# A two-layer graph network: retrieval from the memory computed one stage later, beside the sums of the same state

## The chip, the cores and the metric

The kernel runs on one core of a Trainium2 chip. The core has TensorE (matmuls, results in PSUM), VectorE, ScalarE, GpSimd and SyncE; in the profile they are PE (weight loads: PEld), DVE, ACT, POOL and SP. Each works through its own queue of instructions in order. Transfers run on 16 DMA engines and are issued from the queues of SP, ACT (plain copies) and POOL (gathers with a list of indices). The time is that of one execution on the device, in microseconds (us).

## The reference

32768 nodes with 128 features, 524288 edges (`src`, `dst`). Layer 0 is a graph layer with attention, layer 1 is three steps of a memory layer; the change touches layer 1 alone:

```python
for _ in range(T):                                   # T = 3, ALPHA = 0.5, coeff = 0.2
    q = x @ Wq.T + bq
    attn = softmax(BETA * (q @ keys.T), axis=-1)     # 512 keys
    retrieved = attn @ values
    lap = _laplacian_term(x, row, col)               # x - dinv * sum over edges of dinv * x
    x = (1.0 - ALPHA) * x + ALPHA * (retrieved - coeff * lap)
mu = jnp.mean(x, axis=-1, keepdims=True); var = jnp.var(x, axis=-1, keepdims=True)
return (x - mu) * rsqrt(var + EPS) * ln_w + ln_b
```

After it x is the layer norm of (x1 + this), x1 being layer 1's input. Of a state x, a step thus needs two things that don't depend on each other: the retrieval (with 0.4 x, called `part` in the kernel) and the sum over the edges. The next state is `part` plus that sum.

## The kernel before

A block is 512 nodes (64 blocks), a window 128 nodes (256 windows, four in a block). Every fp32 row is split into three bf16 rows, so that the sums over edges run as bf16 matmuls.

The edges are handled in two halves. **Spread**: for each window of source rows, six groups of matmuls with a 0/1 matrix `pick` (line 1448) copy the rows into slots, two PSUM banks a group; each group is cast to `y_o` (line 1453) by ScalarE or, for every `share`-th group, by VectorE, and half a window is stored to DRAM (line 1456, SP). **Sums**: for each window of target rows, 19 matmuls accumulate in PSUM (`add`, line 1486, matmul at 1495): five with rows gathered by GpSimd (`listed`, line 1470), two with shared gathered rows (`common`), twelve with slots loaded from DRAM (`y_i`, line 1461). The 0/1 matrix `oh` for them is a comparison on VectorE (line 1481). When a window's sums are done, VectorE adds them to `part` (`close`, line 2174, three operations at 2179).

`Sums.steps` (line 1520) gives the order within a window: ask for the slots and gathers `lead` windows ahead, first add, `oh` for a later window, then the other adds, with one extra function after every fourth add where the caller hands some in, and `close` at the end.

Layer 1 has four stages:

1. *First spreads* (pool `l1p`, line 2209). Layer 0's output is normalized (`first`), stored to `xs_d[0]`, multiplied with `dinv` and split (`prepare`, line 2068), and spread (`emit`, line 2094; `share` 2, two PSUM buffers `exp`). The retrieval for the same state runs beside it.
2. and 3. *Middle stages* (pool `l1w`, line 2234), t = 0 and 1: sums of state t (`consume`, line 2165), and, two blocks behind, preparation, spreads and retrieval of the new state t + 1. `weave` (line 1041) mixes the two lists of steps.
4. *Last stage* (pool `l1z`, line 2259): sums of state 2 and the two layer norms at the end (`finish`, line 2187), whose four pieces for the block before go as the extra functions, one in each window: moments; normalize, scale, shift and add x1; moments; normalize and store.

The retrieval of a block is `project` (transposes), `query` (matmul with Wq), four times `scores` (matmul with the keys, maximum on VectorE at line 1061, Exp on ScalarE at 1063) and `turn` (transposes, copy to `pt`), `retrieve` (matmul with the values) and `remain` (transposes, division, 0.4 x, store of `part` to `part_d`). Their places within the 24 steps of a block's spreads are numbers beside them (line 2147). In the stages with sums, `ask_part` (line 2154) loads `part` a block ahead on ScalarE's queue.

In stages 1 to 3 a scheduler orders each engine's instructions around this; in the last stage the order is the written one:

```python
with tc.manual_schedule():                       # line 2264
    ask_part(t, 0, wp)
    sums = Sums(exs[t], wp, p_g, ramp, 6, 2)     # lead 6, oh two windows ahead
    ends = []
    for b in range(NB):
        st = {}
        run(consume(t, b, st, sums, wp, ends))
        ends = finish(b, st, wp)
    run(ends)
```

Of the kernel before, what the change touches and what calls it, by code (L numbers as in the profile page):

```python
# [28 lines left out]
AHEAD = 2  # L29
UNROLL = 4  # L30
# [879 lines left out]
def tile_gnn_resnorm(ctx: ExitStack, tc: tile.TileContext, a: dict, out: bass.AP):  # L910
# [1100 lines left out]
    def layer1_grid(v_d, s3, c3):  # L2011

        exs = [Exchange("src", slots_d[t % 2], rows_d[t]) for t in range(T_STEPS)]
        with tc.tile_pool(name="l1g", bufs=1) as gp:
# [53 lines left out]
            def prepare(t, b, st, wp, p_s, p_tr):  # L2068

                ex = exs[t]  # L2070

                def rows():
                    nx = wp.tile([P, NCH, D], F32, name="nx")
                    nc.vector.tensor_tensor(nx, st["x"], dinv[:, b * NCH:(b + 1) * NCH].unsqueeze(2)
                                            .to_broadcast([P, NCH, D]), OP.mult)
                    st["r"], st["split"] = ex.split_steps(wp, b, nx, nx)

                def project():
                    ps = p_tr.tile([P, NCH, P], F32, name="tr")
                    for c in range(NCH):  # L2080
                        nc.tensor.transpose(ps[:, c, :], st["x"][:, c, :], ident)
                    st["xT"] = wp.tile([P, BLK], F32, name="xT")
                    nc.scalar.copy(st["xT"], ps.rearrange("p c n -> p (c n)"))

                def query():
                    ps = p_s.tile([P, BLK], F32, name="s")
                    nc.tensor.matmul(ps, w["WqT"], st["xT"], start=True, stop=True)
                    st["q"] = wp.tile([P, BLK], F32, name="qT")
                    nc.scalar.activation(st["q"], ps, AF.Identity, bias=v["L1_gnn_bq"])
                return [(1, rows), (2, project), (4, lambda: st["split"][0]()), (7, query),  # L2090
                        (8, lambda: st["split"][1]()), (10, lambda: st["split"][2]()),
                        (14, lambda: st["split"][3]())]

            def emit(t, b, st, wp, p_e, p_s, p_tr, share):

                ex = exs[t]
                y = {}

                def scores(c):
                    if c == 0:  # L2100
                        st["pt"] = wp.tile([P, NCH, BLK], F32, name="pt")
                        st["sums"] = wp.tile([P, NCH], F32, name="sums")
                    s = p_s.tile([P, BLK], F32, name="s")
                    nc.tensor.matmul(s, st["q"][:, c * P:(c + 1) * P], keysT, start=True, stop=True)  # L2104
                    st["pr", c] = softmax_rows(wp, s, st["sums"][:, c:c + 1])
# [19 lines left out]
                def remain():  # L2125
                    ps = p_tr.tile([P, NCH, P], F32, name="tr")
                    for c in range(NCH):
                        nc.tensor.transpose(ps[:, c, :], st["oT"][:, c * P:(c + 1) * P], ident)
                    part = wp.tile([P, NCH, D], F32, name="part_o")
                    nc.vector.tensor_tensor(part, ps, st["rec"].unsqueeze(2).to_broadcast([P, NCH, D]), OP.mult)  # L2130
                    nc.vector.scalar_tensor_tensor(part, st["x"], 0.4, part, op0=OP.mult, op1=OP.add)
                    nc.sync.dma_start(kept_of(part_d, b), flat(part))

                def spread(n):
                    c, m = divmod(n, KS)
                    i = b * NCH + c
                    if m == 0:
                        ask_pick(wp, i + 2)
                    ex.spread(wp, p_e, "exp", i, picked[i], st["r"][:, c, :], m, y, n % share == share - 1)
                    if m == KS - 1:  # L2140
                        del picked[i]

                places = [(n, lambda n=n: spread(n)) for n in range(NCH * KS)]
                return places + [(0, lambda: scores(0)), (3, lambda: scores(1)), (5, lambda: turn(0)),
                                 (6, lambda: scores(2)), (8, lambda: turn(1)), (9, lambda: scores(3)),
                                 (11, lambda: turn(2)), (13, lambda: turn(3)), (17, retrieve), (20, remain)]

# [4 lines left out]
            parts = {}  # L2152

            def ask_part(t, b, wp):

                if b < NB:
                    p_i = wp.tile([P, NCH, D], F32, name="part_i", bufs=3)
                    nc.scalar.dma_start(flat(p_i), kept_of(part_d, b))
                    parts[b] = [p_i]
                    if t == T_STEPS - 1:  # L2160
                        x1 = wp.tile([P, NCH, D], F32, name="x1", bufs=3)
                        nc.scalar.dma_start(flat(x1), kept_of(xs_d[0], b))
                        parts[b].append(x1)

            def consume(t, b, st, sums, wp, extra=()):

                extra = list(extra) + [None] * NCH

                def begin():
                    ask_part(t, b + 1, wp)  # L2170
                    st["part"], *st["x1"] = parts.pop(b)
                    st["x"] = wp.tile([P, NCH, D], F32, name="xn", bufs=5)

                def close(ps, c):
                    i = b * NCH + c
                    acc = st["part"][:, c, :]
                    for o in range(3):
                        dst = st["x"][:, c, :] if o == 2 else acc
                        nc.vector.scalar_tensor_tensor(dst, ps[:, o * D:(o + 1) * D], dinv01[:, i:i + 1],  # L2179
                                                       acc, op0=OP.mult, op1=OP.add)  # L2180

                steps = [begin]
                for c in range(NCH):
                    steps += sums.steps(b * NCH + c, lambda ps, c=c: close(ps, c), [extra[c]] if extra[c] else [])
                return steps

            def finish(b, st, wp):
# [8 lines left out]
                def sum_up():  # L2196
                    st["a"][1]()
                    nc.vector.tensor_add(st["x2"], st["x2"], st["x1"][0])
# [10 lines left out]
            with tc.tile_pool(name="l1p", bufs=2) as wp, \  # L2209
                    tc.tile_pool(name="l1p_exp", bufs=2, space=PSUM) as p_e, \  # L2210
                    tc.tile_pool(name="l1p_s", bufs=2, space=PSUM) as p_s, \
# [4 lines left out]
                for n in range(-NCH - 3, NB):  # L2216
# [10 lines left out]
                    if 0 <= n + 1 < NB:  # L2227
                        lists.append(prepare(0, n + 1, sts[n + 1], wp, p_s, p_tr))
                    if n >= 0:
                        lists.append(emit(0, n, sts[n], wp, p_e, p_s, p_tr, 2))  # L2230
# [3 lines left out]
            with tc.tile_pool(name="l1w", bufs=2) as wp, \  # L2234
# [4 lines left out]
                for t in range(T_STEPS - 1):  # L2239
                    sums = Sums(exs[t], wp, p_g, gc["iota1"], 2)  # L2240
                    sts = {}
                    ask_part(t, 0, wp)
                    for w0 in range(2):
                        ask_pick(wp, w0)
                    for n in range(-2, NB):
                        lists = []
                        if n + 1 in sts:
                            lists.append(prepare(t + 1, n + 1, sts[n + 1], wp, p_s, p_tr))
                        if n >= 0:
                            lists.append(emit(t + 1, n, sts[n], wp, p_e, p_s, p_tr, 4))  # L2250
                        two_b = placed(*lists)
                        b = n + 2
                        if b < NB:
                            sts[b] = {}
                            weave(two_b, consume(t, b, sts[b], sums, wp))
# [3 lines left out]
            with tc.tile_pool(name="l1z", bufs=2) as wp, \  # L2259
                    tc.tile_pool(name="l1z_r", bufs=1, space=PSUM) as p_r, \  # L2260
                    tc.tile_pool(name="l1z_seg", bufs=4, space=PSUM) as p_g:
                t = T_STEPS - 1
                ramp = ramp_in_psum(p_r)
                with tc.manual_schedule():
                    ask_part(t, 0, wp)
                    sums = Sums(exs[t], wp, p_g, ramp, 6, 2)
                    ends = []
                    for b in range(NB):
                        st = {}
                        run(consume(t, b, st, sums, wp, ends))  # L2270
# [91 lines left out]
```

## Time and profile before

| what | value |
| --- | --- |
| median of 3 runs | 13194.35 us (13187.15 to 13196.0) |
| profiled execution, its time | 13193.95 us |
| its span, first to last instruction | 13192.2 us |
| busy in the span: PE, DVE, ACT, POOL | 11231.3, 9517.9, 6589.1, 6302.2 us |
| first spreads, about 5725 to 7180 us | 1455 us |
| middle stages, to 9345 and to 11504 us | 2165 and 2159 us |
| last stage, to the end | 1688 us |

The stages' bounds are read from the first and last instructions of their lines. The shares of busy time over the whole span are averages over stages with different limits, so that each stage is read for itself. A group in the profile is named by its line, its engine, its operation and the tiles it writes and reads (out<-in); "idle before" is the time that the engine stood still just before these instructions, with what it waited for. In the timeline the first number is the start, the second the duration.

### The profile page before, as it was taken

Reading aid. Unit: us, or ns where it says so; the run is one execution under the profiler, and the core shown is the slowest. Engines: PE = TensorE matmul, PEld = TensorE weight load, DVE = VectorE, ACT = ScalarE, POOL = GpSimd, SP = SyncE. Lnnn points to the kernel's source line nnn. Section 1 sums busy time; section 2 is a strip of 40 time slices with the busy share of each in tenths; the row PEclk is TensorE's granted clock in tenths of the full one; section 3 lists DMA queues with packets and bytes.
Section 4 is the critical chain, followed back from the end, with each engine's and each line's share of the span. In section 5 each row is a group of like instructions: output and inputs, shape, how many; then the busy total and the mean of one; then the engine's idle time right before and its main releaser. Section 6 shows DMA issues by size and latency. Waiting matters only on the chain. (4 is left out here: it accounts for less than half of the span.)

```text
span 13192.2 us, 164703 instructions
## 1 busy us (share of the span) xinstructions
PE 11231.3 (85%) x57831; PEld 5536.4 (42%) x57831; DVE 9517.9 (72%) x15195; ACT 6589.1 (50%) x10238; POOL 6302.2 (48%) x5525
## 2 busy tenths in 40 slices
PE   7798798666679988889997999999899999866666
PEld 2233233232334444344443555555455555433333
DVE  7977977899777777678886666666566666566666
ACT  4455455677712222368885666666566666500000
POOL 0084075000077777300001666666566666477777
PEclk9999899999889999999999999999999999988888
DMA  1000000688899999778887999999999999988887
GB/s 43 10 15 19 10 14 16 252 321 323 324 307 316 322 319 320 254 259 309 305 311 293 396 400 400 399 397 397 352 400 398 396 401 399 363 299 290 289 290 255
DMA packets 1410558, 3689.71 MB, mean 280 GB/s; under 512 B 219827, under 2 KB 634707, under 8 KB 1408563
## 3 DMA queue, kind: packets, MB, share of 16 engines
q1 hardware_dynamic: 969712, 2969.23, 59.8%
q0 software_dynamic: 252608, 520.41, 12.5%
q10 hardware_dynamic: 187394, 189.42, 4.4%
q8 instruction: 457, 7.49, 0.2%
q14 instruction: 387, 3.16, 0.1%
HBM read 2175.76 MB, written 1502.58 MB: 279 GB/s over the span
## 5 line engine op out<-in xcount | busy, mean ns | idle before, releaser
L1470 POOL DMA_INDIRECT listed<-rows,other x5120 | 5291.4, 1033 | 4127.8 <-issue 3138.3
L1453 ACT CAST y_o<-exp 128x768 bf16<-128x768 f32 x4224 | 3234.0, 805 | 1162.2 <-PE exp L1448 784.7
L1495 PEld LDWEIGHTS <-oh 128*128 128x128 bf16 x19456 | 1970.8, 102 | 2570.0 <-issue 1529.6
L1448 PE MATMUL exp<-rows,pick 128*128 128x384 bf16 x10752 | 2426.5, 328 | 380.3 <-ACT y_o L1453 223.2
L1495 PE MATMUL seg<-y_i,oh 128*128 128x384 bf16 x12288 | 2563.4, 345 | 20.4 <-DMA y_i<-slots 19.7
L1453 DVE CAST y_o<-exp 128x768 bf16<-128x768 f32 x1920 | 1831.8, 954 | 690.5 <-PE exp L1448 559.1
L1495 PE MATMUL seg<-listed,oh 128*128 128x384 bf16 (+1 forms) x5120 | 1313.3, 335 | 801.7 <-DMA listed<-rows,other 780.5
L1448 PEld LDWEIGHTS <-pick 128*128 128x128 fp8e4 x10752 | 1045.7, 98 | 1729.8 <-issue 1162.7
L1661 ACT ACTIVATE pT<-s 128x1024 f32<-128x1024 f32 x1024 | 1048.4, 1025 | 1378.5 <-PE s L1636 957.5
L1641 DVE TENSOR_REDUCE mx<-s 128x2 f32<-128x1024 f32 x1024 | 1246.3, 1221 | 358.4 <-PE s L1636 357.9
L2179 DVE SCALAR_TENSOR_TENSOR part_i<-seg,dinv,part_i 128x128 f32<-128x128 f32 x1536 | 532.4, 347 | 1337.9 <-PE seg L1495 1319.2
L1657 PE MATMUL s<-ql,k 32*128 32x512 f32 x4096 | 1217.9, 673 | 167.8 <-DVE mx L1641 154.6
L1636 PE MATMUL s<-k,q 32*128 32x512 f32 x4096 | 1222.5, 676 | 9.3 <-DVE mx L1641 4.9
L1481 DVE TENSOR_TENSOR oh<-iota,slot 128x2432 bf16<-128x2432 bf16 x768 | 1087.3, 1416 | 3.0 <-DMA slots<-y_o 3.0
L1084 ACT ACTIVATE ln_rs<-ln_mv,eps_c 128x4 f32<-128x4 f32 x128 | 38.0, 297 | 1637.7 <-DVE ln_mv L1082 1637.7
L2104 PE MATMUL s<-keysT,qT 128*128 128x512 f32 x1536 | 793.7, 598 | 2.0 <-ACT pr L1063 1.4
L2116 PE MATMUL s<-pt,values 128*128 128x512 f32 x1536 | 720.4, 594 | 2.1 <-ACT pt L2111 2.0
L1495 PE MATMUL seg<-common,oh 128*128 128x384 bf16 (+1 forms) x2048 | 607.9, 350 | 50.9 <-DMA common<-rows,shared 50.8
L1657 PEld LDWEIGHTS s<-ql,k 32*128 32x128 f32 x4096 | 320.7, 191 | 763.2 <-DVE mx L1641 314.5
L1392 POOL MEMSET rows<- 128x8 bf16 x64 | 6.7, 106 | 1260.4 <-PE exp L1448 749.7
L1061 DVE TENSOR_REDUCE nm<-s 128x1 f32<-128x512 f32 x768 | 523.6, 684 | 105.6 <-PE s L2104 103.7
L1063 ACT ACTIVATE pr<-s,nm 128x512 f32<-128x512 f32 x768 | 536.3, 698 | 114.9 <-DVE nm L1061 112.1
(410 smaller groups left out, 14178.5 us busy)
## 6 DMA issues: line engine op xcount, KB each, us to landing
slots<-y_o SPq DMA_DIRECT2D x2048, 576.0 KB
y_i<-slots SPq DMA_DIRECT2D x1024, 1152.0 KB
pick<-pick SPq DMA_DIRECT2D x1024, 192.0 KB
listed<-rows,other POOLq DMA_INDIRECT x5120
rows<-rows SPq DMA_DIRECT2D x192, 384.0 KB
band<-row_dst SPq DMA_DIRECT2D x128, 384.0 KB
band<-row_src ACTq DMA_DIRECT2D x256, 192.0 KB
part_d<-part_o SPq DMA_DIRECT2D x192, 256.0 KB
```

Source lines behind the costliest of these rows:

```text
L1063: nc.scalar.activation(pr, s, AF.Exp, bias=nm, accum_out=sums)
L1448: nc.tensor.matmul(ps[:, j, :ROW], pick[:, o:o + P], r, start=True, stop=True)
L1453: (nc.vector.tensor_copy if to_dve else nc.scalar.copy)(dst, ps[:, :, :ROW])
L1470: nc.gpsimd.indirect_dma_start(out=g[:, k, :], out_offset=None, in_=self.table, in_offset=bass.IndirectOffsetOnAxis(ap=index[:, k:k + 1], ...
L1481: nc.vector.tensor_tensor(oh.rearrange("p c (w z) -> p c w z", z=2), ramp.rearrange("p (w z) -> p w z", z=2)[:, None].to_broadcast([P, NC2 ...
L1495: nc.tensor.matmul(ps[:, :n], oh[:, j, :], src, start=(k == 0), stop=(k == NC2 - 1))
L1636: nc.tensor.matmul(ps[:, s % 2, :], t["q", o][32 * s:32 * s + 32, c * P:(c + 1) * P], t["k", o][32 * s:32 * s + 32, :], start=True, stop=True)
L1641: nc.vector.tensor_reduce(m[:, c, 2 * i:2 * i + 2, xr[o]], st[b].pop(("two", i)), AX.X, OP.max, negate=True)
L1657: nc.tensor.matmul(ps[:, s % 2, :], t["k", o][32 * s:32 * s + 32, c * P:(c + 1) * P], t["ql", o][32 * s:32 * s + 32, :], start=True, stop= ...
L1661: nc.scalar.activation(t["p", c][:, 2 * i:2 * i + 2, :], ps, AF.Exp)
L2104: nc.tensor.matmul(s, st["q"][:, c * P:(c + 1) * P], keysT, start=True, stop=True)
L2116: nc.tensor.matmul(ps, values[:, k, :], st["pt"][:, k, :], start=(k == 0), stop=(k == NCH - 1))
```

## The change

The retrieval for state t leaves the stage that makes state t and goes to the stage that sums it: out of the first spreads, from state t + 1 to state t in the middle stages, and new into the last stage. Its functions are the same; they are taken out of `prepare` and `emit` into `memory`, which gives a front (`project`, `query`) and a back (the rest).

- Each middle and last stage loads the states themselves (`ask_state`, `x_i`, three blocks ahead, on ScalarE's queue), from `xs_d[0]`, `part_d` and `xs_d[1]`, and the middle stages store the state that they finish (`close`, on SP's queue) where `remain` stored `part`. `part` stays on the chip.
- Before the first block of a stage `first_states` computes the whole retrieval of block 0 and the front of block 1. From then on, beside the sums of block b, stand the back of block b + 1 and the front of block b + 2 (`ahead`).
- In the first spreads the PSUM banks of the retrieval go to a third `exp` buffer, and every third cast is VectorE's (before: every second).
- In the last stage there are 16 places in a block, one after every fourth add; the pieces of the layer norms stand first in places 0, 4, 8 and 12, the steps of the retrieval at two thirds of their old numbers. The PSUM buffers of the sums go from 4 to 3, two each go to the retrieval's `s` and `tr`, and slots and gathers are asked for 5 windows ahead and not 6.

```diff
-            def prepare(t, b, st, wp, p_s, p_tr):
+            def prepare(t, b, st, wp):
...
+            def memory(st, wp, p_s, p_tr, bufs):
                 def project():
                     ps = p_tr.tile([P, NCH, P], F32, name="tr")
                     for c in range(NCH):
-                        nc.tensor.transpose(ps[:, c, :], st["x"][:, c, :], ident)
+                        nc.tensor.transpose(ps[:, c, :], st["xi"][:, c, :], ident)
...
-                    part = wp.tile([P, NCH, D], F32, name="part_o")
+                    st["part"] = part = wp.tile([P, NCH, D], F32, name="part")
                     nc.vector.tensor_tensor(part, ps, st["rec"].unsqueeze(2).to_broadcast([P, NCH, D]), OP.mult)
-                    nc.vector.scalar_tensor_tensor(part, st["x"], 0.4, part, op0=OP.mult, op1=OP.add)
-                    nc.sync.dma_start(kept_of(part_d, b), flat(part))
+                    nc.vector.scalar_tensor_tensor(part, st["xi"], 0.4, part, op0=OP.mult, op1=OP.add)
+
+                return ([(2, project), (7, query)],
+                        [(0, lambda: scores(0)), (3, lambda: scores(1)), (5, lambda: turn(0)),
+                         (6, lambda: scores(2)), (8, lambda: turn(1)), (9, lambda: scores(3)),
+                         (11, lambda: turn(2)), (13, lambda: turn(3)), (17, retrieve), (20, remain)])
...
+            states = [xs_d[0], part_d, xs_d[1]]
+            def ask_state(t, b, wp, p_s, p_tr):
                 if b < NB:
+                    st = {"xi": wp.tile([P, NCH, D], F32, name="x_i", bufs=3)}
+                    nc.scalar.dma_start(flat(st["xi"]), kept_of(states[t], b))
+                    st["front"], st["back"] = memory(st, wp, p_s, p_tr, 1 if t == T_STEPS - 1 else 2)
+                    mems[b] = st
+            def first_states(t, wp, p_s, p_tr):
+                for b in range(3):
+                    ask_state(t, b, wp, p_s, p_tr)
+                run(f for _, f in mems[0]["front"] + mems[0]["back"] + mems[1]["front"])
+            def ahead(b):
+                lists = [mems[b + 1]["back"]] if b + 1 < NB else []
+                return lists + ([mems[b + 2]["front"]] if b + 2 < NB else [])
...
+                    if c == NCH - 1 and t < T_STEPS - 1:
+                        nc.sync.dma_start(kept_of(states[t + 1], b), flat(st["x"]))
...
-                    tc.tile_pool(name="l1p_exp", bufs=2, space=PSUM) as p_e, \
-                    tc.tile_pool(name="l1p_s", bufs=2, space=PSUM) as p_s, \
+                    tc.tile_pool(name="l1p_exp", bufs=3, space=PSUM) as p_e, \
...
-                        lists.append(emit(0, n, sts[n], wp, p_e, p_s, p_tr, 2))
+                        lists.append(emit(0, n, sts[n], wp, p_e, 3))
...
-                        two_b = placed(*lists)
                         b = n + 2
+                        two_b = placed(*lists, *ahead(b))
...
-                    tc.tile_pool(name="l1z_seg", bufs=4, space=PSUM) as p_g:
+                    tc.tile_pool(name="l1z_s", bufs=2, space=PSUM) as p_s, \
+                    tc.tile_pool(name="l1z_tr", bufs=2, space=PSUM) as p_tr, \
+                    tc.tile_pool(name="l1z_seg", bufs=3, space=PSUM) as p_g:
...
-                    sums = Sums(exs[t], wp, p_g, ramp, 6, 2)
+                    sums = Sums(exs[t], wp, p_g, ramp, LAST, 2)
+                    first_states(t, wp, p_s, p_tr)
...
+                        slots = [[] for _ in range(4 * NCH)]
+                        for c, f in enumerate(ends):
+                            slots[4 * c].append(f)
+                        for at, f in sorted((x for one in ahead(b) for x in one), key=lambda x: x[0]):
+                            slots[at * 4 * NCH // (NCH * KS)].append(f)
+                        extra = [[lambda fs=fs: run(fs) for fs in slots[4 * c:4 * c + 4]] for c in range(NCH)]
+                        run(consume(t, b, st, sums, wp, p_s, p_tr, extra))
```

`LAST` is 5.

## The prediction

> **What bounds the kernel now.** I first cut the span into the stages of layer 1 with the view of busy time by stretch. The rows are the spreads of layer 0 (for comparison), the first spreads of layer 1, the two middle stages and the last stage.
>
> ```profile
> core 0: us, PE busy (x) PEld busy (x) DVE busy (x) ACT busy (x) POOL busy (x), PEclk, DMA share, GB/s
> 2383.00:3622.00 1239.00, 830.86 (x3720) 375.37 (x3720) 1082.30 (x1478) 928.20 (x1317) 12.27 (x68) 0.93 0.88 321
> 5725.00:7180.00 1455.00, 1296.33 (x6016) 688.42 (x6016) 1256.51 (x2320) 1152.98 (x1967) 0.00 (x0) 0.99 0.84 306
> 7180.00:9345.00 2165.00, 2067.13 (x10605) 1155.32 (x10606) 1303.93 (x2109) 1346.24 (x2230) 1400.54 (x1333) 0.99 1.01 390
> 9345.00:11504.00 2159.00, 2070.16 (x10646) 1156.81 (x10644) 1307.59 (x2115) 1359.84 (x2251) 1360.49 (x1291) 1.00 1.01 391
> 11504.00:13192.00 1688.00, 1088.27 (x4864) 540.95 (x4864) 1077.29 (x2880) 39.32 (x129) 1264.36 (x1312) 0.81 0.85 286
> ```
>
> Three different limits show. The first spreads (1455 us) have TensorE at 89%, VectorE at 86%, ScalarE at 79% and transfers at 84%: no single one is full, the engines hand work to each other. The middle stages have full transfers (share 1.01). The last stage has nothing full by these columns, ScalarE almost idle, and a granted clock of 0.81. Next I read the waits of the last stage (waiter, waited for, us in total, times, longest).
>
> ```profile
> DVE part_i L2179 <- PE seg L1495: 547.6, 151, 17.5
> PE seg L1495 <- DMA listed<-rows,other: 532.5, 350, 5.5
> POOL listed L1470 <- issue: 336.6, 1105, 0.3
> ```
>
> TensorE waits for gathered rows, and GpSimd, which issues the gathers, waits for nobody: 0.3 us between one gather and the next. So GpSimd bounds this stage: 1312 gathers at 0.95 + 0.3 = 1.25 us are 1640 us. By the timeline a window of the sums takes 6.50 us here (1456.5 us for 224 windows), a block of four 26.0 us. A window is 19 accumulating matmuls ("adds").
>
> Then the groups of the first spreads (count | busy us, mean ns | idle before), for the prices of what moves:
>
> ```profile
> L1453 DVE CAST y_o<-exp 128x768 bf16<-128x768 f32 x768 | 733.1, 955 | 136.3 <-PE exp L1448 119.9 <-ACT pt L2111 4.0 <-ACT y_o L1453 2.8
> L1453 ACT CAST y_o<-exp 128x768 bf16<-128x768 f32 x768 | 615.3, 801 | 229.4 <-PE exp L1448 195.4 <-ACT xT L2083 9.0 <-DMA slots<-y_o 7.6
> L1063 ACT ACTIVATE pr<-s,nm 128x512 f32<-128x512 f32 x256 | 178.0, 695 | 15.0 <-DVE nm L1061 12.4
> L1061 DVE TENSOR_REDUCE nm<-s 128x1 f32<-128x512 f32 x256 | 174.1, 687 | 40.9 <-PE s L2104 40.0
> L1063 ACT ACT_TABLE_LOAD x16 | 20.5, 1283 | 0.3
> ```
>
> And last the timeline of VectorE over one window of the last stage (start, us, operation), since the change puts work into this queue:
>
> ```profile
> 12330.22 0.74 DVE L2179 SCALAR_TENSOR_TENSOR part_i<-seg,dinv,part_i 128x128 f32<-128x128 f32 x2 [4.73 <-PE seg L1495]
> 12331.00 0.35 DVE L2179 SCALAR_TENSOR_TENSOR xn<-seg,dinv,part_i 128x128 f32<-128x128 f32 x1
> 12331.26 1.42 DVE L1481 TENSOR_TENSOR oh<-ramp_p,slot 128x2432 bf16<-128x2432 bf16 x1
> 12332.59 0.17 DVE L1088 RECIPROCAL ln_rs<-ln_rs 128x4 f32<-128x4 f32 x1
> 12332.80 1.11 DVE L1090 TENSOR_SCALAR x<-xn,ln_mv,ln_rs 128x128 f32<-128x128 f32 x4
> 12333.95 0.69 DVE L1093 TENSOR_TENSOR x<-x,ln_w 128x512 f32<-128x512 f32 x1
> 12334.67 0.69 DVE L1094 TENSOR_TENSOR x<-x,ln_b 128x512 f32<-128x512 f32 x1
> 12335.40 0.69 DVE L2198 TENSOR_TENSOR x<-x,x 128x512 f32<-128x512 f32 x1
> 12336.01 0.73 DVE L2179 SCALAR_TENSOR_TENSOR part_i<-seg,dinv,part_i 128x128 f32<-128x128 f32 x2
> ```
>
> The reader is to see an order that can't be swapped: the close of a window waits for its last add, then come the comparison `oh` (1.33 us to the next start) and a piece of the layer norms (here 3.42 us), and only then anything that stands behind them.
>
> **The change, part by part.** The profiled execution took 13193.95 us (span 13192.2, 1.75 us around it), 0.4 us below the median of the runs; the sum goes from 13194.
>
> *First spreads.* Away go, per block, 4 reductions of 0.69 us and 1.7 us of remainder on VectorE, 4 Exp of 0.70 + 0.20 and 7 copies or Identity of 0.6 to 0.7 on ScalarE, the matmuls between them, and one 256 KB store on SP's queue. Casts go from 768 : 768 to 1024 on ScalarE and 512 on VectorE. New sums: ScalarE 1024 x 0.801 = 820 plus 52 (vT), 80 (rows) and 5 (square root) = 957; VectorE 512 x 0.955 = 489 plus about 353 (norm, moments, rows) = 842; TensorE under 700. Transfers: 0.84 x 1455 = 1222 us of engine time for 446 MB; without the 64 stores (16.8 MB) 1176. So the transfers become the floor. How near does the stage come? The middle stages reach a share of 1.01, which gives 1164; the layer 0 spreads, also with three PSUM buffers, 0.88, which gives 1336; with no better coupling than now it is 1400. Layer 0's VectorE was 87% busy, here it would be near 67%, so I take a share of 0.93, 1265 us: **-190** (ends -291 and -55).
>
> *Middle stages.* The same retrieval runs, on the state that is summed and not the one that is spread; 64 loads of `x_i` for 64 of `part_i` on ScalarE's queue, 64 stores of the state for 64 of `part_d` on SP's, both waiting for the same kind of VectorE result. Transfers stay full, so the middle costs nothing either way; if the transfers had room, TensorE at 95% would still hold it. The edges change: after the last sums the last two blocks are spread, 53 us from 11449.8 to 11502.9, with retrieval in it (ScalarE 26 us a block, without it 16): -20 each. At the start one retrieval stands ahead of the sums, partly in the 20 us in which the first rows are gathered: +5 to +15 each. Together **-25** (ends -50 and +20).
>
> *Last stage.* Added per block on TensorE: 4 score groups of 0.85 us (two passes, 1.02 with the drain of 0.17), one query of 0.85, 6 groups of transposes of 0.43, one retrieval of 3.42 = 10.3 us beside 76 adds of 0.16 (12 take 2.11) = 12.3. In sum 22.6 us for a block, less than GpSimd's 26.0. VectorE gets 4 x 0.69 + 0.3 + 1.4, together 1370 of 1688 us. ScalarE gets 10 us and, as square root and Exp now alternate in every block, two table loads of 1.28. By sums GpSimd would go on bounding it.
>
> By order it doesn't. The stage's order is written out by hand, and the built program keeps it: in VectorE's queue each reduction for Exp stands behind the close, `oh` and the norm piece of its window, and TensorE, behind four of its adds, waits in three windows of four for what comes of it. Queued behind that wait are the rest of the window's adds, whose end the next close waits for. So a block is one chain, counted from TensorE's last add of the block before:
>
> - Window 0: VectorE still has the remainder of the retrieval (1.6 past that add), close 1.04, `oh` 1.33, moments 1.6; ScalarE square root 0.3, table load 1.28 (the reduction hides beside it), Exp 0.9; TensorE, which waited some 3.5 us at the first turn: 0.43, 3 adds 0.49, drain 0.17. With handoffs of 0.04: 9.2.
> - Window 1: close 1.04, `oh` 1.33, norm 3.42, reduction 0.69, Exp 0.9; the fourth scores wait for a PSUM buffer of two that this Exp frees (3.4 us of wait), then 0.85, 4 adds 0.65, turn 0.43, 3 adds 0.49, drain 0.17: 10.1.
> - Window 2: close 1.04, `oh` 1.33, moments 1.6; on ScalarE the square root 0.3 stands ahead of the copy 0.6 that the retrieval needs; TensorE 3.42, 3 adds 0.49, drain: 9.1.
> - Window 3: only TensorE, 19 adds and a turn: 3.5.
>
> Sum 31.9 us against 26.0. It holds 10.8 us of TensorE at full clock. The clock was 0.81 in this stage with TensorE waiting a third of the time, 0.93 in the layer 0 spreads (67% busy), 0.99 at 89%; here it would be busy 22.6 of 32, so I take 0.9: +1.2, of which 0.4 is lost in VectorE's overhang of 1.6. 32.7 - 26.0 = 6.7, times 64 blocks: **+430**. Ends: at full clock with the table load hidden 31.0, +320; at 0.81 33.6, +490. A buffer of gathers less (5 windows ahead for 6) costs nothing, since GpSimd is then ahead of TensorE.
>
> [...]
>
> Sum: 13194 - 190 - 25 + 430 = 13409, say **13410 us**, 1.6% slower.
>
> **Rivals.**
>
> 1. *GpSimd goes on bounding the last stage (faster).* For it: TensorE's 22.6 us and VectorE's 21 fit into 26.0. It decides if a block's chain is below 26.0, 6 us shorter than counted, as when reductions don't really stand behind the norms. Against it: the order. Then the last stage costs only its start, some 15 us: 13194 - 190 - 25 + 15 = 12994. The kernel would be faster up to a block of 29.4 (215 / 64 = 3.4 us more).
> 2. *The first spreads hardly gain*, because the transfers' waits take the place of the casts' (ScalarE waited 83 us for stores in 800 us of the layer 0 spreads): -55 for -190, 13545.
> 3. *The clock falls further*, to the 0.73 that the profile shows in the 60 us after 7180, where TensorE also waits again and again: 10.8 us become 14.8, the overhang of 1.6 is gone, 34.3 us a block, +530: 13509.
>
> That the change doesn't do what it says is excluded by the built order.
>
> **How the numbers follow.** The forecast gets 0.76: the durations are measured and queues keep their order, but a chain of 20 links can be wrong in one. Rival 1 gets 0.13, rival 2 0.07, rival 3 0.04. The forecast's own terms, not all at their ends together, span 13210 to 13540. The range 13205 to 13545 leaves out rival 1 and a few hundredths at the ends. What differs by 0.2% (26 us) is about what a measurement can tell from no change. Faster takes rival 1, 0.13; slower 0.85; 0.02 for a chain near 29.4.
>
> **What would show it.** In the profile after: the first spreads near 1265 us with a DMA share above 0.9; middle stages near 2150; the last stage near 2120, with GpSimd now waiting for TensorE's adds, TensorE waiting for Exp (first turn, fourth scores) and for the copy ahead of the retrieval, some 3 us each once a block, and ScalarE with 128 table loads. Wrong it is if TensorE still waits there for gathered rows.

## The result, and the profile after

The kernel after takes 13551.47 us (median of four runs, 13527.14 to 13573.62), the kernel before 13190.75 us beside it (13186.14 to 13196.0): a ratio of 1.027 with a 95% interval of 1.0258 to 1.0282. It is slower, as forecast, by 361 us where 216 were forecast; the time lies 6 us above the range.

The profiled execution took 13573.62 us with a span of 13571.8, which is 22 us above the median. The busy time by stretch, cut at the stages of layer 1 (first spreads, two middle stages, last stage; columns as in the prediction's first fence):

```profile
5753.00:7005.00 1252.00, 817.30 (x3328) 374.00 (x3328) 789.96 (x1553) 887.16 (x1232) 0.00 (x0) 0.82 0.94 342
7005.00:9190.00 2185.00, 2082.35 (x10675) 1165.04 (x10676) 1311.54 (x2123) 1359.33 (x2257) 1371.85 (x1325) 0.99 1.01 385
9190.00:11362.00 2172.00, 2066.46 (x10574) 1146.93 (x10573) 1303.05 (x2102) 1351.38 (x2224) 1346.23 (x1300) 0.99 1.01 389
11362.00:13572.00 2210.00, 1714.40 (x7552) 949.54 (x7552) 1334.46 (x3393) 626.71 (x1213) 1265.34 (x1312) 0.90 0.65 219
```

The first spreads now have a transfer share of 0.94 (before 0.84). The middle stages look as they did, but for the last column: 385 and 389 GB/s where the rows of before have 390 and 391. The last stage, 2210 us where it was 1688, has a transfer share of 0.65 (0.85) and GpSimd busy for 57% of it (75%).

To compare stages of several kernels, I cut all traces at the same instructions: the first and the last matmul of the spreads (`exp`) of layer 1's first state, the last cast before the last stage, and the end of the span. A block in the last stage is the mean over 56 of the 64.

| us | up to the first spreads | first spreads | middle stages | last stage | a block in it |
| --- | --- | --- | --- | --- | --- |
| before | 5748.6 | 1428.0 | 4327.3 | 1688.3 | 26.03 |
| after | 5776.6 | 1224.7 | 4361.5 | 2209.1 | 34.38 |
| difference | +28.0 | -203.3 | +34.2 | +520.8 | +8.35 |

The differences sum to 379.7 us, the difference of the two spans. The 28 us lie in work that the change doesn't touch. In the nine other kernels profiled below, all of which leave it alone too, it takes 5744.5 to 5767.7 us, so that it varies between executions; it is about the distance of this execution from the median.

The waits of the last stage of after (waiter, waited for, us in total, times, longest):

```profile
DVE part L2194 <- PE seg L1496: 661.4, 188, 6.5
POOL listed L1471 <- PE seg L1496: 548.5, 176, 5.5
ACT pr L1064 <- DVE nm L1062: 483.1, 125, 6.9
PE tr L2124 <- ACT pr L1064: 219.3, 63, 4.0
PE s L2118 <- ACT pr L1064: 136.3, 61, 3.3
PE s L2130 <- ACT pt L2125: 111.1, 62, 1.9
```

They answer to the three lines of before, in which TensorE waited for gathered rows and GpSimd for nobody. Now GpSimd waits for TensorE's adds. The last three lines are one wait a block each: TensorE for the first Exp (3.5 us), for the PSUM buffer that an Exp frees (2.2 us), for the copy ahead of the retrieval (1.8 us). Then the timeline of VectorE and of TensorE over the first window of one block (start, us, operation, idle before):

```profile
12516.93 1.41 DVE L1482 TENSOR_TENSOR oh<-ramp_p,slot 128x2432 bf16<-128x2432 bf16 x1
12518.26 0.28 DVE L1082 BATCH_NORM_STATS2 ln_st<-xn 128x6 f32<-128x128 f32 x1
...
12519.76 0.18 DVE L1083 BATCH_NORM_AGGREGATE ln_mv<-ln_st 128x2 f32<-128x6 f32 x1
12519.86 1.25 DVE L1062 TENSOR_REDUCE nm<-s 128x1 f32<-128x512 f32 x2
```

```profile
12518.39 0.81 PE L1496 MATMUL seg<-y_i,oh 128*128 128x384 bf16 x4
12522.72 1.12 PE L2124 MATMUL tr<-ident,pr 128*128 128x128 f32 x4 [3.51 <-ACT pr L1064]
12523.63 1.17 PE L1496 MATMUL seg<-y_i,oh 128*128 128x384 bf16 x3
12524.59 1.49 PE L1496 MATMUL seg<-listed,oh 128*128 128x384 bf16 x4
...
12532.17 1.44 PE L2118 MATMUL s<-keysT,qT 128*128 128x512 f32 x2 [2.60 <-ACT pr L1064]
12533.40 1.49 PE L1496 MATMUL seg<-y_i,oh 128*128 128x384 bf16 x4
```

The first fence is the order that the forecast rests on: `oh`, the moments, and only then the reduction. The second shows what follows: TensorE waits 3.51 us, and the matmuls right behind the wait run at half speed: four adds take 1.49 us where the four ahead of the wait take 0.81. These four already belong to the next window; on the chain lie the turn and the three adds ahead of them, which take 1.87 us from start to start (12522.72 to 12524.59) where the same ones take 0.98 in experiment 4. The last two lines, from the next window, show half speed on the chain again, behind the 2.60 us that the fourth scores wait: four adds in 1.49 us.

### The profile page after: what moved, and what is told of

The parts are those of the page before. It is cut to its first block, busy times and chain, and to the rows that moved or that the text cites. A ratio compares the mean times of both kernels' runs of the same rounds, so it can differ in the third digit from the quotient of the medians.

```text
span 13571.8 us, 165045 instructions
## 1 busy us (share of the span) xinstructions
PE 11406.4 (84%) x57831; PEld 5639.9 (42%) x57831; DVE 9310.5 (69%) x14939; ACT 6916.3 (51%) x10588; POOL 6270.6 (46%) x5525
## 4 chain that ended last, share of the span: by engine, by line
PE 37%; DVE 24%; DMA 17%; POOL 10%; ACT 7%; issue 5%; ACTq 0%; SPq 0%; DVEq 0%; POOLq 0%
DMA slots<-y_o 11%; PE seg L1496 10%; PE exp L1449 10%; POOL listed L1471 5%; ACT y_o L1454 4%; DVE y_o L1454 3%; PE s L2118 3%; DMA listed<-rows,other 3%; PE s L2130 3%; DVE mx L1642 3%; DVE oh L1482 2%; PE s L1658 2%; PE tr L2124 2%; DMA y_i<-slots 2%; POOL moved L661 1%
## 5 line engine op out<-in xcount | busy, mean ns | idle before, releaser
L1454 ACT CAST y_o<-exp 128x768 bf16<-128x768 f32 x4480 | 3383.9, 805 | 1244.2 <-PE exp L1449 786.0
L1449 PE MATMUL exp<-rows,pick 128*128 128x384 bf16 x10752 | 2580.0, 348 | 751.3 <-ACT y_o L1454 358.6
L1496 PEld LDWEIGHTS <-oh 128*128 128x128 bf16 x19456 | 1939.4, 100 | 1890.0 <-issue 903.9
L1496 PE MATMUL seg<-y_i,oh 128*128 128x384 bf16 x12288 | 2530.4, 335 | 14.3 <-DMA y_i<-slots 13.6
L1454 DVE CAST y_o<-exp 128x768 bf16<-128x768 f32 x1664 | 1587.1, 954 | 1010.0 <-PE exp L1449 806.5
L1449 PEld LDWEIGHTS <-pick 128*128 128x128 fp8e4 x10752 | 1095.6, 103 | 2080.6 <-issue 1394.0
L2194 DVE SCALAR_TENSOR_TENSOR part<-seg,dinv,part 128x128 f32<-128x128 f32 x1536 | 533.2, 347 | 1378.2 <-PE seg L1496 1366.3
L1637 PE MATMUL s<-k,q 32*128 32x512 f32 x4096 | 1217.9, 675 | 10.1 <-ACT pT L1662 5.6
L2118 PE MATMUL s<-keysT,qT 128*128 128x512 f32 x1536 | 839.8, 629 | 139.3 <-ACT pr L1064 138.2
L2124 PE MATMUL tr<-ident,pr 128*128 128x128 f32 x3072 | 542.2, 290 | 223.2 <-ACT pr L1064 222.9
```

Of the source, the lines that this page charges most:

```text
L1449: nc.tensor.matmul(ps[:, j, :ROW], pick[:, o:o + P], r, start=True, stop=True)
L1454: (nc.vector.tensor_copy if to_dve else nc.scalar.copy)(dst, ps[:, :, :ROW])
L1496: nc.tensor.matmul(ps[:, :n], oh[:, j, :], src, start=(k == 0), stop=(k == NC2 - 1))
L1637: nc.tensor.matmul(ps[:, s % 2, :], t["q", o][32 * s:32 * s + 32, c * P:(c + 1) * P], t["k", o][32 * s:32 * s + 32, :], start=True, stop=True)
L2124: nc.tensor.transpose(ps[:, k, :], st["pr", c][:, k * P:(k + 1) * P], ident)
```

## The experiments

Two theories for the last stage stood at the start. **A**, the forecast's: the order in VectorE's queue (reduction behind a norm piece) makes the chain. **B**, on top of it: TensorE does the chain's own matmuls behind its waits at half rate, as in the fence above (four adds in 1.49 us for 0.81 behind 3.51 us), so that the mean clock of 0.90 understates the loss.

### 1. The norm pieces three places later

```diff
-                            slots[4 * c].append(f)
+                            slots[4 * c + 3].append(f)
```

> The changed kernel with the four layer norm pieces of the last stage moved from the first to the last place of their window (places 3, 7, 11, 15 for 0, 4, 8, 12); same work, same instructions. Theory A (the order in VectorE's queue makes a block of the last stage one chain of 33.8 us): the reductions for Exp then stand right behind the comparison, the chain of a block falls below GpSimd's 26.0 us, the last stage goes back to 1690 to 1750 us, total about 13050 to 13110, faster than the kernel before. Rival C (the last stage is long because TensorE, VectorE or the gathers have too much to do there): the order changes nothing, 13500 to 13570.

Measured: 13022.74 us (12998.16 to 13039.03, four runs), a ratio to before of 0.9859 (0.9839 to 0.9878). The last stage takes 1696.6 us, a block 26.11. The waits of the last stage, and VectorE's timeline over a first window:

```profile
POOL listed L1471 <- issue: 336.2, 1103, 0.3
...
PE tr L2124 <- ACT pr L1064: 122.4, 61, 3.0
...
DVE part L2194 <- PE seg L1496: 107.3, 123, 4.2
```

```profile
12304.49 1.41 DVE L1482 TENSOR_TENSOR oh<-ramp_p,slot 128x2432 bf16<-128x2432 bf16 x1
12306.01 0.69 DVE L1062 TENSOR_REDUCE nm<-s 128x1 f32<-128x512 f32 x1
```

The reduction follows `oh`, the close's wait falls from 661 to 107 us, and GpSimd waits for nobody again. One index is worth 529 us by the medians (512 in the last stage), and the change with it is 1.4% faster than the kernel before. The stage lies in the range expected under theory A, the total 27 us below its range. Theory A holds: the order, not the amount of work, made the loss.

### 2. The same places, the norm piece behind the retrieval's step

```diff
                         slots = [[] for _ in range(4 * NCH)]
-                        for c, f in enumerate(ends):
-                            slots[4 * c].append(f)
                         for at, f in sorted((x for one in ahead(b) for x in one), key=lambda x: x[0]):
                             slots[at * 4 * NCH // (NCH * KS)].append(f)
+                        for c, f in enumerate(ends):
+                            slots[4 * c].append(f)
```

> The changed kernel with the norm pieces in the same places 0, 4, 8, 12 of the last stage, but behind the retrieval's step of that place. Theory A: the reductions of the first and third scores no longer stand behind a norm piece; square root and Exp still alternate, with two more table loads a block; last stage 1690 to 1850 us, total 13050 to 13210. Rival C: 13500 to 13570.

Measured: 13058.4 us (one run), the last stage 1733.8, a block 26.70. Nothing but the order of the pieces within a place differs from after, and 7.7 of the 8.35 us a block go.

### 3. A third PSUM buffer for `s`

```diff
-                    tc.tile_pool(name="l1z_s", bufs=2, space=PSUM) as p_s, \
+                    tc.tile_pool(name="l1z_s", bufs=3, space=PSUM) as p_s, \
...
-                    tc.tile_pool(name="l1z_seg", bufs=3, space=PSUM) as p_g:
+                    tc.tile_pool(name="l1z_seg", bufs=2, space=PSUM) as p_g:
```

> The changed kernel with three PSUM buffers for scores, query and retrieval in the last stage, and two for the sums instead of three. Theory A: the fourth scores no longer wait for the third Exp, but the third turn, three steps later, waits for the same Exp; 1 to 2 us less a block, last stage 2080 to 2150 us for 2210, total 13430 to 13500. If PSUM buffers were the cause and not the order, the whole wait of 2.2 us a block and what hangs on it would go and the stage would fall to 2050 or less. Rival C: no change.

Measured: 13305.36 us (one run), the last stage 1987.5, a block 30.74. That is 3.6 us a block less than after, more than the 1 to 2 of theory A. The wait of `s` for Exp is gone from the list of waits, and the granted clock of the stage rises:

```profile
11316.00:13303.00 1987.00, 1556.09 (x7552) 866.80 (x7552) 1336.64 (x3392) 612.90 (x1213) 1269.23 (x1312) 0.97 0.73 243
```

By the bound set beforehand the buffer would be the cause; experiments 1 and 2 say otherwise, since with two buffers and another order the block is 26.1 and 26.7. The buffer matters only as long as the reductions come late. Most of the 3.6 us isn't the buffer's own wait either: experiment 4, with the clock at 0.99 and also two PSUM buffers for the sums, has a block of 32.25, so that the third buffer for `s` is worth about 1.5 us (32.25 to 30.74), within the 1 to 2 of theory A. The other 2.1 are half rate that went with it, though the wait ahead of the first turn stayed:

```profile
12327.16 0.66 PE L2124 MATMUL tr<-ident,pr 128*128 128x128 f32 x4 [3.52 <-ACT pr L1064]
12327.65 0.65 PE L1496 MATMUL seg<-y_i,oh 128*128 128x384 bf16 x3
12328.14 0.81 PE L1496 MATMUL seg<-listed,oh 128*128 128x384 bf16 x4
```

Behind the same 3.52 us the matmuls run at full speed here, four adds in 0.81 us. By the trace's record of the granted clock half rate follows this wait in 22 of 61 blocks, in after in 61 of 61. In these two kernels the length of the wait alone thus doesn't decide the rate; what else does was not tried.

### 4. Filler matmuls in the waits

```diff
+                def warm(n):
+                    for _ in range(n):
+                        nc.tensor.matmul(idle, gc["ident"], some, start=True, stop=True)
...
-                        for at, f in sorted((x for one in ahead(b) for x in one), key=lambda x: x[0]):
-                            slots[at * 4 * NCH // (NCH * KS)].append(f)
+                        fill = [(4.9, lambda: warm(15)), (8.9, lambda: warm(11)), (16.9, lambda: warm(8))]
+                        for at, f in sorted((x for one in ahead(b) + [fill] for x in one), key=lambda x: x[0]):
+                            slots[int(at * 4 * NCH // (NCH * KS))].append(f)
```

The sums' PSUM buffers are two here as in experiment 3; `idle` is a bank of its own.

> The changed kernel with matmuls into an unused PSUM bank (their result is not used) ahead of the first turn, the fourth scores and the retrieval of each block in the last stage: 15, 11 and 8 of 0.16 us, 2.4, 1.8 and 1.3 us of TensorE time, which fill most of its three waits of 3.9, 2.2 and 1.8 us; the sums get two PSUM buffers for three. Theory B (what the forecast missed in the last stage, 33.8 us a block for 32.7, is that TensorE runs at half rate behind each of its waits, on the very matmuls that the chain needs): the granted clock of the stage goes from 0.90 to 0.97 or more and the block to about 32 us, the last stage to 2060 to 2130 us, although TensorE has 350 us more to do. If the rate is not the reason, or TensorE's work is: the stage stays at 2210 or grows to 2300 and more.

Measured: 13410.31 us (one run), the last stage 2086.1, a block 32.25, and the clock of the stage 0.99. TensorE's timeline, first turn of a block:

```profile
12319.14 2.60 PE L2288 MATMUL idle<-slot,ident_b 128*128 128x384 bf16 x15
12322.82 0.66 PE L2124 MATMUL tr<-ident,pr 128*128 128x128 f32 x4 [1.08 <-ACT pr L1064]
12323.31 0.65 PE L1496 MATMUL seg<-y_i,oh 128*128 128x384 bf16 x3
12323.80 0.81 PE L1496 MATMUL seg<-listed,oh 128*128 128x384 bf16 x4
```

More work on TensorE makes the kernel 2.13 us a block faster. The turn still waits for Exp, but the four adds behind it take 0.81 us again, not 1.49. Theory B holds beside A: the half rate is worth 2.13 us a block, 123 us of the stage (2209.1 to 2086.1). The sums' two PSUM buffers for three were not run by themselves.

### 5. No square root in the last stage, two `exp` buffers in the first spreads

Two edits in two stages, each read from its own stage.

```diff
-                    tc.tile_pool(name="l1p_exp", bufs=3, space=PSUM) as p_e, \
+                    tc.tile_pool(name="l1p_exp", bufs=2, space=PSUM) as p_e, \
...
-            nc.scalar.activation(t["rs"], mv[:, :, 1], AF.Sqrt, bias=eps_c)
+            nc.scalar.activation(t["rs"], mv[:, :, 1], func, bias=eps_c)
```

`func` is `AF.Identity` for the two layer norms of `finish` and `AF.Sqrt` elsewhere.

> The kernel after, with one edit in each of two stages, which are read apart by stage. (1) First spreads: two `exp` buffers again, with every third cast still on VectorE. With three it takes 1219 to 1225 us in five profiles. If the third buffer is a part of the gain, the stage takes 1260 to 1330; if the retrieval's leaving did it alone, 1235 or less. (2) Last stage: the square root of the two layer norms is left out (ScalarE copies the variance plus epsilon in its place), so that the tables are never switched; the output is that of these norms without a root. By the chain, the table load ahead of Exp stands in window 0 and is partly beside VectorE's reduction (0.69 us): 0.9 us of 1.28 are on the chain, 58 us in the stage, which falls from 2209 to about 2150. If the load is hidden, 2195 or more; if it lies on the chain whole with the half rate that its wait brings, 2110 or less.

Measured (one run, 13515.06 us): first spreads 1307.4 us, last stage 2097.2, a block 32.61.

```profile
5737.00:7070.00 1333.00, 919.66 (x3328) 366.00 (x3328) 791.55 (x1552) 914.50 (x1232) 0.00 (x0) 0.82 0.89 321
...
11416.00:13513.00 2097.00, 1663.07 (x7552) 913.20 (x7552) 1336.11 (x3392) 461.73 (x1088) 1268.21 (x1312) 0.92 0.69 231
```

The third buffer is worth 83 us of the first spreads (transfer share 0.89 without it, 0.94 with it). The table load that Exp waits for costs 1.77 us a block, 112 us, more than its own 1.28: it lies on the chain whole, since the wait of the first turn goes from 219.3 to 140.9 us in 63 blocks, 1.24 us each; the clock rises from 0.90 to 0.92 with it. The expected 0.9 us was too little, because the reduction is done when the load begins: in after the load starts behind a wait of 0.32 us for `nm`.

### 6. Every second cast on VectorE, three `exp` buffers

```diff
-                        lists.append(emit(0, n, sts[n], wp, p_e, 3))
+                        lists.append(emit(0, n, sts[n], wp, p_e, 2))
```

> The kernel after with every second cast of the first spreads on VectorE, as before, and three `exp` buffers. VectorE then has 768 x 0.955 + 353 = 1086 us of work in the stage, ScalarE 752. If transfers are what is left as the floor, the stage takes 1225 to 1260 us (it took 1219 to 1225 in five profiles); if the split of the casts is what let it reach the floor, 1290 or more. The last stage is unedited and shows how far a second profile of it repeats 2209 us.

Measured: 13514.36 us (one run); the first spreads take 1178.1 us, less than the change's own 1224.7 and less than expected:

```profile
5740.00:6945.00 1205.00, 814.05 (x3328) 375.37 (x3328) 1015.55 (x1808) 715.92 (x976) 0.00 (x0) 0.83 0.97 356
```

VectorE is busy 84% of the stage and ScalarE 59%, and the transfers come to a share of 0.97. With three buffers the new split of the casts was thus no part of the gain but a loss of 46 us (35 to 47 over all profiles of both splits, experiment 8 being the second with this one). The unedited last stage repeats: 2218.9 us, a block 34.53.

### 7. Block 0's retrieval in the stage before

On the kernel of experiment 1; the core of the edit:

```diff
-                run(f for _, f in mems[0]["front"] + mems[0]["back"] + mems[1]["front"])
+                if t:
+                    mems[0] = early.pop()
+                else:
+                    run(f for _, f in mems[0]["front"] + mems[0]["back"] + mems[1]["front"])
...
-                        two_b = placed(*lists, *ahead(b))
+                        two_b = placed(*lists, *ahead(b, t), *next_first(t + 1, n, wp, p_s, p_tr, gp))
```

`next_first` hands out the front and the back of block 0 of state t + 1 beside blocks 22 and 23 of stage t.

> The kernel with the layer norms behind the retrieval's step (first experiment), and the retrieval of block 0 of the next state moved out of the start of a stage: it is done in the stage before, at blocks 22 and 23, into buffers of its own, for the second middle stage and the last stage; the front of block 1 goes into block 0. The start of these two stages then needs only the first rows. If the retrieval is what makes 28 us of the 11 from the last cast to the first sum, both starts fall back to 9 to 14 us: 30 to 35 us less in all, a median near 12990 us. If the loads of the state or the gathers make it, the starts stay at 25 or more and the time at 13020.

Measured: 13016.92 us (13005.06 to 13038.89, four runs), a ratio to before of 0.986 (0.9844 to 0.9876): no different from experiment 1. The last stage does begin earlier, 11.7 us from the last cast to the first add where it was 28.4 (before: 10.7), and takes 1684.3 us for 1696.6. The middle stages give nothing back: 4360.7 us against 4344.6, in a set of profiles of this change that goes from 4344.6 to 4361.5. So the wait at the start of the last stage is the retrieval's, some 12 to 17 us; what a retrieval at the start of a middle stage costs is less than this spread of 17 us can show.

### 8. The best of them together

On the kernel of experiment 7, with the early block 0 for the last stage alone and `emit(0, n, sts[n], wp, p_e, 2)`.

> The kernel with the layer norms behind the retrieval's step (first experiment), with every second cast of the first spreads on VectorE, and the retrieval of the last stage's block 0 done in the stage before (for the last stage alone). By the stages measured one by one, the first spreads take 1178 us in place of 1221 and the last stage 1685 in place of 1697, the rest stays: 55 us less than the 13023 of the first experiment, a median near 12968. If what the first spreads save is given back in the middle stages, which begin with more transfers outstanding, near 13010.

Measured: 12989.59 us (12968.89 to 12992.04, five runs), a ratio to before of 0.9841 (0.9828 to 0.9855). The first spreads take 1181.6 us, the last stage 1687.0, the middle stages 4360.3. The first two are as expected; the middle, 16 us above that of experiment 1, is at the upper end of what it takes in other profiles, and whether it took these 16 us from the first spreads isn't settled. This version is faster than after, and 1.6% faster than before.

### 9. The middle stages without the retrieval

On the kernel of experiment 1:

```diff
                     st["front"], st["back"] = memory(st, wp, p_s, p_tr, 1 if t == T_STEPS - 1 else 2)
+                    if t < T_STEPS - 1:
+                        def keep(st=st):
+                            st["part"] = wp.tile([P, NCH, D], F32, name="part")
+                            nc.vector.tensor_scalar(st["part"], st["xi"], 0.4, None, op0=OP.mult)
+                        st["front"], st["back"] = [], [(20, keep)]
```

> The kernel of the first experiment without the retrieval in the two middle stages (`part` is 0.4 x alone there, so that the output is another; the state is loaded as before, by the same transfers). The forecast held that full transfers set these stages whatever stands beside them. If so, they stay within 30 us of the 4345 of the first experiment, and the order of the retrieval can't be the reason for the 17 to 34 us that they gained. If the retrieval's work on TensorE and ScalarE holds them too, they fall to 4250 or less (it is some 16 us of TensorE in each of 128 blocks).

Measured: 13106.51 us (one run). Neither side expected it: without the retrieval the middle stages are slower, 4446.0 us for 4344.6. Both middle stages in one stretch, of before, of experiment 1 and of this kernel:

```profile
7177.00:11504.00 4327.00, 4137.30 (x21249) 2312.13 (x21249) 2612.05 (x4225) 2706.08 (x4480) 2761.03 (x2624) 0.99 1.01 390
```

```profile
6989.00:11333.00 4344.00, 4138.72 (x21249) 2310.04 (x21249) 2613.65 (x4225) 2710.98 (x4482) 2713.68 (x2624) 0.99 1.01 389
```

```profile
6966.00:11412.00 4446.00, 3209.32 (x15873) 1600.57 (x15873) 2193.99 (x3329) 1897.07 (x2561) 2854.87 (x2624) 0.93 1.01 380
```

In all three the transfers have a share of 1.01, and time by rate is the same amount: 4327 x 390, 4344 x 389 and 4446 x 380 all come to 1687 to 1690 MB. What differs is how fast they move at this share: 390, 389 and 380 GB/s. One line of the waits within the first middle stage (1900 us of experiment 1, then 2000 us of this kernel) shows where the slower one differs:

```profile
ACT y_o L1454 <- DMA slots<-y_o: 101.4, 86, 5.5
```

```profile
ACT y_o L1454 <- DMA slots<-y_o: 729.2, 165, 11.4
```

Without the retrieval in its queue ScalarE runs ahead with the casts and waits for its stores. Why the transfers then move less per microsecond was not tried.

## Why the prediction was right or wrong

The direction, the place and the mechanism of the last stage were right. Two terms of the sum were too low, the middle stages and the half rate in the last stage, and together they put the time above the range.

- **First spreads, -190 forecast, -203 measured: right in size, partly by luck.** The transfers came to a share of 0.94, for 0.93 taken, but not to their floor: experiment 6 reaches 0.97 and 1178 us, near the 1164 by the middle stages' share. The reason given for 0.93, a VectorE that would be only 67% busy, doesn't hold, since in experiment 6 it is 84% busy and the stage shorter. By experiments 5 and 6 two things made the gain: with the retrieval out, the new split of the casts and two buffers still, the stage went from 1428 to 1307 us, and the third buffer brought 83 more. The working weighed the sums of casts on each engine and left out what the third in three costs, 46 us here.
- **Middle stages, -25 forecast, +34 measured in this execution (+17 to +34 in the profiles of this change with the retrieval in it): wrong.** The step that failed is "Transfers stay full, so the middle costs nothing either way". They stay full, and taking the retrieval away doesn't shorten the stage (experiment 9), but the full share of 1.01 didn't fix a rate here: 385 GB/s for 390 and 389 for 391 are 1.3% and 0.5%, some 28 and 11 us of the two stages. The edges failed too: the last spreads after the sums shortened by 5 us in the second stage (53.1 to 47.6) and lengthened by 1 in the first (61.3 to 62.7), for 20 each. What lowers the rate stays open. Before was profiled once, and its runs spread over 10 to 28 us within a set, so that the +17 at the lower end isn't clear of noise; the forecast gain of 25 is in none of the profiles.
- **Last stage, +430 forecast, +521 measured: the mechanism right, one term mis-sized.** The order makes the chain (experiments 1 and 2), and the table load lies on it whole, as counted (experiment 5); only the reduction doesn't hide beside the load, which waits for it (below). With the clock at 0.99 a block takes 32.25 us (experiment 4) against 31.9 counted at full clock. The step that failed is "so I take 0.9: +1.2, of which 0.4 is lost in VectorE's overhang": the mean clock was 0.90, but the slow pieces in after are those behind a wait (1.49 us for 0.81), and behind a wait is where the chain runs. The half rate costs 2.13 us a block, not 0.8. From the last add of one window to that of the next, as the forecast counted, the four windows take 10.0, 11.1, 9.8 and 3.5 us (means of 56 blocks) for 9.2, 10.1, 9.1 and 3.5 counted; in experiment 4, at a clock of 0.99, they take 9.4, 10.2, 9.1 and 3.5. So each window of the count was within about 0.2 us, and the loss lies in the three windows in which TensorE waits.
- **The rivals.** GpSimd doesn't go on bounding the last stage in after; it does as soon as the order lets it (experiment 1, 13023 us, near the 12994 of that rival). The first spreads gained in full, against the second rival. The third rival, a clock of 0.73, didn't come either: the mean stayed at 0.90, and the loss came from where in the block the slow pieces lie.
- **The sum.** Against the forecast: -13 in the first spreads, +59 in the middle, +91 in the last stage. That is +137 of the 141 us between 13410 and the median; the 28 us of unchanged work and the 22 us by which this execution lies above the median nearly cancel.

The trace of after has half rate behind every wait of 3.5 us, and behind shorter waits too, while experiment 3 has waits of 3.5 us without it. By the record of the granted clock there are 112 stretches at half rate in 56 blocks of after, nearly all of 3.41 us: one in each block behind the first turn's wait, the other behind the fourth scores' wait (36 blocks, median 2.4 us) or the retrieval's (20 blocks, 1.9 us). If the chain ran on TensorE all through both stretches, half of each would be lost, 3.41 us a block or 218 over 64, an estimate from these lengths. Experiment 4's 2.13 us are 136 over 64 blocks and the forecast had 51, so the truth lay between: a part of each stretch falls on matmuls off the chain, such as the four adds of the next window in the result's fence.

A table load takes 1283 ns in after, in the mean of the 62 ahead of Exp, and Exp starts 0.02 us after the load (below). Experiment 5 saved 1.77 us a block, of which the load is 1.28; the turn's wait fell by 1.24.

ScalarE's timeline in the same window of after:

```profile
12519.97 0.30 ACT L1085 ACTIVATE ln_rs<-ln_mv,eps_c 128x4 f32<-128x4 f32 x1 [8.86 <-DVE ln_mv L1083]
12520.59 1.28 ACT L1064 ACT_TABLE_LOAD   x1 [0.32 <-DVE nm L1062]
12521.89 0.69 ACT L1064 ACTIVATE pr<-s,nm 128x512 f32<-128x512 f32 x1
```

## What to carry to other kernels

In an order written by hand, look at what stands in each queue ahead of the one instruction that another engine waits for: here the same work, with short reductions ahead of long norm pieces, is 529 us faster, and the busy sums had been right all along that it fits. Where a chain runs through TensorE and the trace shows half rate behind waits, work out a block with the pieces behind them at the reduced rate too, and not by the stage's mean clock alone. Full transfers didn't move at one rate here: at a share of 1.01 the same amount took 4327 to 4446 us, so leave a few per cent for it.

## What the runs showed of the hardware

- Behind waits of 3.5 us TensorE ran at half rate in every block of after (four adds 1.49 us for 0.81), but only in 22 of 61 blocks of experiment 3; behind waits of 1.9 us it did so in 20 of 56 blocks of after. Filling the waits with useless matmuls raised the clock of the stage from 0.90 to 0.99 and made it 123 us faster (2209.1 to 2086.1).
- Transfers at a share of 1.01 moved 380 to 391 GB/s; with a quarter of TensorE's matmuls taken away the two middle stages took 101 us more.
- A table load on the chain cost 1.77 us a block (experiment 5), 0.5 more than the 1.28 it lasts.
